# Two graph layers on one core: more direct rows on VectorE, list matrices and setup copies on ScalarE, square roots instead of powers from block 10, and the second product kept in two tensors

## The chip, the cores and the metric

The kernel runs on one core of one Trainium2 chip. The metric is the device time of one launch in microseconds (us). A core has five engines that each work through their own instructions in order: TensorE (PE in the profile, its weight loads PEld), VectorE (DVE), ScalarE (ACT), GpSimd (POOL) and SyncE (SP). Transfers between device memory and on-chip memory are started by SP or POOL and carried by 16 shared DMA engines.

## The reference

Two graph layers follow each other on 2708 nodes with 512 features. The adjacency matrix is dense in memory (2708 x 2708 float32), but only about 0.3% of it and its diagonal are nonzero.

```python
# layer 0
rowsum = adj.sum(axis=1)
d = where(rowsum > 0, rowsum ** -0.5, 0)
x = layernorm(x + relu(((d[:, None] * adj * d[None, :]) @ x) @ W + b))
# layer 1, four heads; A_self and A_neigh drop out of the softmax (they add one number to a whole row)
t = x @ W_node + b_node
feats = einsum('nd,hdf->hnf', t, K)
attn = softmax(s[:, :, None] - 1e10 * (1 - adj))        # over the neighbours
x = layernorm(x + relu(mean_h(attn @ feats)))
```

Because of the factor 1e10 a row's softmax puts all weight on its largest adjacency entry. Layer 1 is therefore one row of `u = h @ M + c` per node, where `h` is layer 0's output, `M` is `W_node @ mean(K)`, and the row is that of the largest entry. A check at the end branches to a dense version if the data break the assumptions; it doesn't run here.

## The kernel before, in words

The nodes are 21 full blocks of 128 rows and one of 20 rows. All instructions are placed by hand in one order (`manual_schedule`); on each engine they run in that order, each waiting for what it needs.

**Setup.** For each block `i` the program loads 128 rows of `adj` (1.35 MB, into one of 9 slots) and of `x`. `turn` transposes `x` on TensorE and a copy brings the result to on-chip memory (`sT`, line 219); `times` multiplies by `W`. `diagonal` (line 304, POOL) zeroes the diagonal, `sum_rows` (line 292, ACT) sums the rows, `root` makes `dinv` on POOL with a power. `value` (line 526) scales the product and stores it as `v_d`. `find` (lines 311 and 312, DVE) finds the eight largest entries of a third of each row, so that there are three searches a block. After a block's third search `under_0` (line 298, ACT) reads it a last time, and its slot is free for another load. 43 of the 66 searches stand before the main loop, the others within its first blocks. `weights` (line 490) makes `M` on TensorE.

**Lists.** For each block and each third, the largest entry is the *direct* one; the rest go into lists. `hot` (lines 392 and 397, DVE), `enlist` (line 410, TensorE) and `listed` (lines 422 to 426, DVE) compact the rest into six lists of up to 128 entries: a column, a row and a value each.

**Main loop.** Blocks 0 to 20 have nine chunks each, in the order direct, list, list, three times. For a chunk, POOL gathers 128 rows of `v_d` by an indirect DMA into a tile `g` (`fetch_chunk`, line 596). `small_matrix` makes a 128 x 128 matrix `s`: for a direct chunk a diagonal, on ACT (line 626), for a list chunk a matrix with one entry a row, on DVE (line 631). TensorE adds `s` times `g` to `acc` (`add_chunk`, line 650). In blocks of `BY_VECTOR` (11 to 17) the direct chunks have no matrix and no product: DVE adds the scaled `g` to the block's own row tile `vs` (line 640). Matrices are made, and gathers issued, 11 chunks ahead of use; after block 11 the gathers run up to 22 chunks ahead. There are 12 tiles `g`, and 12 more (`g2`) from block 8 on.

At a block's end `norm_1` (lines 682 to 702) adds up, adds `x` and starts the layer norm. Below block 17 (`EARLY`) `spread` and `norm_2` make the inverse root with a power on POOL (line 707), `nbs` follows on ACT (line 711), and `norm_3` scales on ACT (line 730). From block 17 on `root_1` and `root_2` make it from ACT's square root and four small DVE operations (lines 716 to 725). Chunk 2 of the next block finishes the norm; chunk 7 transposes `h` (`turn_h`), and chunk 5 of the block after that makes its `u` (`u_product`, line 228, then `u_store`, line 764). `u` is stored whole in `u_d`, and blocks 0 to 16 also in `u_e`.

**Rows that don't fit.** Some 128 rows with more entries than the lists hold are gathered whole (`l_a`) in block 10 and multiplied densely, block by block: `listed_turn` (line 959), its copy `l_t` on ACT (line 961), `listed_product` (line 968). They are handled as a block `L` of their own.

**Layer 1.** When `u` of blocks 0 to 16 and of `L` is there, `y_fetch` (line 1000, POOL) gathers each node's row of `u_e`; `y_1` (line 1012, DVE), `y_2` (line 1017, ACT), `root_1`, `root_2` and `y_3` finish the norm, and the block is stored. These pieces (`pieces_y`) are spread over the last chunks and the end. Nodes whose row lies in blocks 17 to 20 are *late*: their `h` is gathered from `h_d` (`to_read`), their `u` from `u_d` (`top_l`), and they are put into the output by indirect stores (`to_put`).

Of the kernel before, what the change touches and what calls it, by code (L numbers as in the profile page):

```python
# [39 lines left out]
F32 = mybir.dt.float32  # L40
# [15 lines left out]
DIRECT = 1  # L56
BY_VECTOR = range(11, 18)
FOUND = 7
# [3 lines left out]
def tile_two_graph_layers(  # L62
# [51 lines left out]
    v_d = dram.tile([N, D], F32, name="v_d")  # L114
    u_d = dram.tile([N, D], F32, name="u_d")
    u_e = dram.tile([EARLY * P, D], F32, name="u_e")
    h_d = dram.tile([N // P * P, D], F32, name="h_d")

# [300 lines left out]
    def listed(ib):  # L419

        t = search.tile([P, NL, 6], F32, name="sheet", bufs=6)
        nc.vector.tensor_copy(t, sheets.pop(ib)[:, : NL * 6].rearrange("p (n c) -> p n c", c=6))  # L422
        col = search.tile([P, NL], U32, name="l_col", bufs=6)
        val = search.tile([P, NL], F32, name="l_val", bufs=6)
        nc.vector.scalar_tensor_tensor(col, t[:, :, 1], float(P), t[:, :, 2], op0=ALU.mult, op1=ALU.add)
        nc.vector.tensor_reduce(val, t[:, :, 3:], axis=AX.X, op=ALU.add)
        lists[ib] = t[:, :, 0], col, val

# [93 lines left out]
    def value(i):  # L522

        pr = rows(i)
        vt = wpool.tile([P, D], F32, name="vt", bufs=3)
        nc.scalar.activation(vt[:pr], pos_w.pop(i)[:pr], AF.Copy, scale=dinv[:pr, i : i + 1])
        store(v_d, vt, i, nc.gpsimd if i < NB - 3 else nc.sync)
        if i == 0:
            nc.gpsimd.dma_start(out=u_d[full:N, :], in_=vt[: N - full])

# [7 lines left out]
    for i in range(NB):  # L538
# [3 lines left out]
        if i + 1 < NB:  # L542
            search_for(i + 1)
            diagonal(i + 1)
            xT[i + 1] = turn(xs.pop(i + 1), rows(i + 1), nc.vector.tensor_copy)
        pos_w[i] = times(xT.pop(i), pr, w_sb, po=p_acc.tile([P, D], F32, name="acc"))
# [6 lines left out]
        if 10 <= i < 10 + ND:  # L553
            turn_weight(i - 10)
        elif i == 15:
            b_columns()
        elif i == NB - 2:
            c_row = bias_1()
        elif i == NB - 1:
            pieces(c_3, c_row)  # L560
        for _ in range(2 if i else 1):
            if finds[0][0] <= i and len(finds) > 3 * (NB - 12):
                search_next()
# [28 lines left out]
    def by_vector(ib, c):  # L592
        return ib in BY_VECTOR and CHUNKS[c][0] == "d"

# [23 lines left out]
    def small_matrix(ib, c):  # L618
# [10 lines left out]
        else:  # L629
            row, _, val = lists[ib]  # L630
            nc.vector.tensor_scalar(  # L631
# [38 lines left out]
    def own_term(ib):  # L670

        pr = rows(ib)
        vs = own[ib][0]
        if not bias_on_pe(ib):
            nc.vector.scalar_tensor_tensor(
# [3 lines left out]
    def norm_1(n, pr, t, ac, vs, xr):  # L679

        if bias_on_pe(n):
            nc.vector.scalar_tensor_tensor(
# [6 lines left out]
        )  # L689
        if n < EARLY:  # L690
            spread(n, pr, t, xr)
        else:
            s = slice(n, n + 1)
            nc.vector.tensor_scalar(nms[:pr, s], tot[:pr, s], -1.0 / D, None, op0=ALU.mult)
            nc.scalar.activation(xr[:pr], t[:pr], AF.Square, bias=nms[:pr, s], accum_out=sqs[:pr, s])

# [59 lines left out]
    def u_store(ib):  # L756
# [10 lines left out]
        elif ib == EARLY - 1:  # L767
            later(1, lambda: put(ut, u_e[:, :], dl["own"][:, ib : ib + 1], EARLY * P))
        if ib >= NS - 2 and ib != L:
            put(ut, u_d[:, :], dl["own"][:, ib : ib + 1])  # L770
        elif ib != L:
            store(u_d, ut, ib)
        u_done.add(ib)
# [140 lines left out]
    def rank_4():  # L914
# [13 lines left out]
        nc.vector.tensor_copy(to_put, other)  # L928
        nc.vector.scalar_tensor_tensor(top_l, t[:, :, 2], float(P), t[:, :, 3], op0=ALU.mult, op1=ALU.add)
        nc.vector.scalar_tensor_tensor(put_own, flag, float(N), own_row, op0=ALU.mult, op1=ALU.add)  # L930
        dl.update(read=to_read, put=to_put, top=top_l, own=put_own)

# [42 lines left out]
    def listed_norm():  # L975
# [5 lines left out]
        )  # L981
        spread(L, P, t, dl["x"])

# [13 lines left out]
    def y_fetch(n):  # L997

        ys[n] = row_space()
        nc.gpsimd.indirect_dma_start(  # L1000
            out=ys[n],
            out_offset=None,
            in_=u_e[:, :],
            in_offset=bass.IndirectOffsetOnAxis(ap=idx[:, n : n + 1], axis=0),
            bounds_check=EARLY * P - 1,
            oob_is_err=False,
        )

    def y_1(n):
        t = h_of[n]  # L1010
        s = slice(n, n + 1)
        nc.vector.scalar_tensor_tensor(t, ys[n], 0.0, t, op0=ALU.max, op1=ALU.add, accum_out=tot[:, s])
        nc.vector.tensor_scalar(nms[:, s], tot[:, s], -1.0 / D, None, op0=ALU.mult)

    def y_2(n):
        s = slice(n, n + 1)
        nc.scalar.activation(ys.pop(n), h_of[n], AF.Square, bias=nms[:, s], accum_out=sqs[:, s])

    def y_3(n):
        (norm_3 if n % 2 else norm_v)(n, P, h_of[n])  # L1020


    GROUP = 3
    n_pieces = NS + 11
    early_y = [[] for _ in range(n_pieces)]
    for n in range(NS):
        last = n // GROUP * GROUP + GROUP - 1
        early_y[n].append(lambda n=n: y_fetch(n))
        early_y[n + 5].append(lambda n=n: (y_1(n), y_2(n)))
        if n == last:  # L1030
            early_y[last + 6].append(lambda n=n: root_1(n - GROUP + 1, n + 1))
            early_y[last + 7].append(lambda n=n: root_2(n - GROUP + 1, n + 1))
        early_y[last + 8 + n % GROUP].append(lambda n=n: (y_3(n), store(out, h_of[n], n)))

    def pieces_y(k):
        for _ in range(k):
            for f in early_y.pop(0) if early_y else ():
                f()


# [37 lines left out]
    for ib in range(NS):  # L1078
        pr = rows(ib)
        listing = []  # L1080
        for c in range(C):
# [17 lines left out]
            if c in (4, 8) and listing:  # L1099
                listed(listing.pop(0))  # L1100
            if finds and c in (1, 4, 7):
                search_next()
# [4 lines left out]
            if found_at is not None:  # L1107
                for f in plan.pop((ib - found_at, c), []):
                    f()
            if c == 2 and ib:  # L1110
                if ib - 1 < EARLY:
                    norm_2(ib - 1, ib, rows(ib - 1))
                    norm_3(ib - 1, rows(ib - 1), space(ib - 1))
                else:
                    root_1(ib - 1, ib)
                    root_2(ib - 1, ib)
                    norm_v(ib - 1, P, space(ib - 1))
                store(h_d, space(ib - 1), ib - 1)
# [5 lines left out]
            for k in sorted(products_u):  # L1124
                u_store(k)
            if c == (5 if ib <= EARLY else 1):
                for k in sorted(hTs):
# [7 lines left out]
            if dl.get("at") == n - 2:  # L1135
                norm_2(L, L + 1, P)
                norm_3(L, P, h_of[L])
                waiting_h.append(L)
            if L in h_of and "at" not in dl:
                dl["at"] = n  # L1140
            if "set" not in dl and u_done >= set(range(EARLY - 1)) | {L}:
                dl["set"] = n
                later(3, lambda: put(dl["u"], u_e[:, :], dl["put"][:, NLATE:], EARLY * P))
            if "go" not in dl and u_done >= set(range(EARLY)) | {L}:
                dl["go"] = n + 4
            if "put_l" not in dl and u_done >= set(range(NS - 2)) | {L}:
                dl["put_l"] = n
                later(4, lambda: put(dl["u"], u_d[:, :], dl["put"][:, NLATE:]))
            if n >= dl.get("go", n + 1) and (n - dl["go"]) % 4 != 3:
                pieces_y(1)  # L1150
            tick()
        if not finds and late is None:
# [9 lines left out]
            nc.scalar.copy(c_bc, po)  # L1162
        if 9 <= ib < 12:

            at = (EARLY - 1, NS - 2, NS - 1)[ib - 9]
            store(u_e if at < EARLY else u_d, space(ib - 9), at)
        if ib + 1 < NS:
# [3 lines left out]
    assert not finds and not plan and not products_l and "go" in dl and hot_next == NS  # L1171
    assert "put_l" in dl and not due and not products_u

    ib = NS - 1
    u_product(ib - 1)
    root_1(ib, ib + 1)
    pieces_y(1)
    root_2(ib, ib + 1)
    norm_v(ib, P, space(ib))
    store(h_d, space(ib), ib)  # L1180
    stir(8)
    turn_h(ib)
    u_store(ib - 1)
    u_product(ib)
    pieces_y(max(3, NS - 1 - (n_pieces - len(early_y))))
    pieces_y(2)
    for k in range(NLATE):
        h_of[L + 1 + k] = row_space()
        fetch(h_of[L + 1 + k], P, dl["read"][:, k : k + 1], h_d[:, :])
        if k == 2:  # L1190
            u_store(ib)
            pieces_y(1)
    pieces_y(2)

    order = [L] + [L + 1 + k for k in range(NLATE)]
    for n in order:
        ys[n] = row_space()
        k = NLATE if n == L else n - L - 1
        fetch(ys[n], P, dl["top"][:, k : k + 1], u_d[:, :])
        pieces_y(1)  # L1200
# [12 lines left out]

    def square(n):
        y_1(n)
        y_2(n)

    for n in order[: half + 1]:
        square(n)
        if n == first[-1]:  # L1220
            root_1(first[0], first[-1] + 1)
    root_2(first[0], first[-1] + 1)
    for n in first:
        y_3(n)
        rows_out(n)
    for n in order[half + 1 :]:
        square(n)
    root_1(second[0], second[-1] + 1)
# [150 lines left out]
```

## Time and profile before

| | us |
|---|---|
| median of 3 runs (512.05 to 519.46) | 513.81 |
| the profiled execution, device time | 516.84 |
| its span, first to last instruction | 515.1 |
| busy: TensorE / VectorE / ScalarE / GpSimd | 420.5 / 375.4 / 244.3 / 335.2 |
| first gather of the main loop issued | 142.7 |
| first product of the main loop | 151.0 |
| last gather of the main loop issued | 430.3 |
| block 20's layer norm begins (VectorE) | 464.4 |
| the last store's issue ends | 509.5 |

The span splits into the setup (to about 150 us), the main loop (to about 465 us) and an end of some 50 us, in which the last `u` is made, stored, and gathered again. A share of busy time over the whole span says little here, since the three have different limits; each is read by itself.

### The profile page before, as it was taken

To read this page: it belongs to the slowest core of one execution; us is meant where nothing else is said; L and a number is where in the kernel's file an instruction comes from. 1 tells how busy PE (TensorE), PEld (TensorE's weight loads), DVE (VectorE), ACT (ScalarE), POOL (GpSimd) and SP (SyncE) were. 2 spreads that over 40 slices of the span, in tenths; PEclk is the share of its full clock that TensorE was granted. 3 is DMA by queue.
4 is the path that set the end of the run, shared out by engine and by line. 5 is a ranking of instruction groups with operands and counts; after the bars stand their busy time and mean duration, and the time that the engine had idled before them with its cause. 6 is when DMAs were issued, how large, how long until landed. Compare 5 with 4: busy or idle time off the path is not lost. (4 is left out here: it accounts for less than half of the span.)

```text
span 515.1 us, 5634 instructions
## 1 busy us (share of the span) xinstructions
PE 420.5 (82%) x1431; PEld 200.9 (39%) x1431; DVE 375.4 (73%) x917; ACT 244.3 (47%) x413; POOL 335.2 (65%) x441
## 2 busy tenths in 40 slices
PE   4969859788979999999998799599898999976000
PEld 3424334343334444444444445244343444433000
DVE  2999999997887988888789938256345454777742
ACT  1598978779642544554532205112222251465631
POOL 6334543453677777777774778888778765745644
PEclk9998999989988999999999989899899799999555
DMA  7999999996276788898895899699899866776862
GB/s 228 424 398 419 396 350 347 372 357 257 93 224 192 234 256 291 302 291 277 267 327 177 267 392 382 212 346 322 284 307 315 300 198 222 238 235 226 296 202 98
DMA packets 54093, 145.79 MB, mean 283 GB/s; under 512 B 10771, under 2 KB 10771, under 8 KB 51216
## 3 DMA queue, kind: packets, MB, share of 16 engines
q0 software_dynamic: 21920, 68.94, 43.5%
q1 hardware_dynamic: 32132, 76.41, 39.3%
q8 instruction: 13, 0.21, 0.2%
q14 instruction: 28, 0.23, 0.1%
HBM read 117.59 MB, written 29.44 MB: 285 GB/s over the span
## 5 line engine op out<-in xcount | busy, mean ns | idle before, releaser
L650 PE MATMUL acc<-g,s 128*128 128x512 f32 x336 | 165.6, 623 | 3.1 <-DMA g<-v_d,l_col 3.1
L596 POOL DMA_INDIRECT g<-v_d,l_col x126 | 134.6, 1069 | 38.0 <-issue 20.4
L650 PEld LDWEIGHTS acc<-g,s 128*128 128x128 f32 x336 | 62.8, 199 | 70.5 <-issue 63.2
L228 PE MATMUL acc<-w_sb,sT 128*128 128x512 f32 (+1 forms) x176 | 85.5, 632 | 0.0
L228 PE MATMUL po<-m_sb,sT 128*128 128x512 f32 x176 | 82.6, 614 | 3.6 <-ACT sT L219 3.6
L596 POOL DMA_INDIRECT g<-v_d,cols x63 | 69.8, 1108 | 22.4 <-issue 10.2
L311 DVE MAX8 vals<-a 128x8 f32<-128x896 f32 (+2 forms) x66 | 71.8, 1088 | 1.0 <-ACT a L292 1.0
L312 DVE FIND_INDEX8 ats<-vals,a 128x8 uint32<-128x896 f32 (+2 forms) x66 | 72.0, 1091 | 0.0
L298 ACT ACTIVATE a<-a 128x2708 f32<-128x2708 f32 (+1 forms) x22 | 54.0, 2457 | 15.9 <-DVE ats L312 15.8
L292 ACT ACTIVATE a<-a 128x2708 f32<-128x2708 f32 (+1 forms) x22 | 54.0, 2456 | 13.4 <-POOL a L304 13.2
L228 PEld LDWEIGHTS po<-m_sb,sT 128*128 128x128 f32 x176 | 34.0, 197 | 46.5 <-issue 41.4
L228 PEld LDWEIGHTS acc<-w_sb,sT 128*128 128x128 f32 (+1 forms) x176 | 33.4, 200 | 36.2 <-issue 36.2
L631 DVE TENSOR_SCALAR s<-place,sheet,l_val 128x128 f32<-128x128 f32 x126 | 40.7, 354 | 4.2 <-PE acc L650 4.1
L219 ACT COPY sT<-tp 128x512 f32<-128x512 f32 x23 | 13.4, 583 | 62.7 <-PE tp L217 62.7
L304 POOL TENSOR_SCALAR_AFFINE_SELECT a<-a 128x128 f32<-128x128 f32 (+1 forms) x22 | 6.5, 295 | 55.8 <-DMA a<-in_adj_dram 49.5
L711 ACT ACTIVATE nbs<-nms,rss 128x1 f32<-128x1 f32 x18 | 5.3, 293 | 67.4 <-POOL rss L707 67.4
L422 DVE COPY sheet<-ls 128x36 f32<-128x36 f32 x21 | 4.0, 192 | 42.7 <-PE ls L410 42.7
L410 PEld LDWEIGHTS <-hot 128*128 128x128 bf16 x378 | 26.7, 161 | 18.3 <-issue 11.0
L217 PE MATMUL tp<-ident,x 128*128 128x128 f32 (+1 forms) x88 | 14.6, 291 | 21.9 <-DMA x<-in_x_dram 17.5
L410 PE MATMUL ls<-either,hot 128*128 128x12 bf16 x378 | 26.0, 203 | 4.7 <-DVE l_sheet L918 2.8
L1000 POOL DMA_INDIRECT g<-u_e,idx x21 | 23.6, 1122 | 7.2 <-issue 4.6
L392 DVE TENSOR_TENSOR hot<-place,places 128x2304 bf16<-128x2304 bf16 x21 | 28.2, 1344 | 0.0
(250 smaller groups left out, 566.7 us busy)
## 6 DMA issues: line engine op xcount, KB each, us to landing
a<-in_adj_dram SPq DMA_DIRECT2D x21, 1354.0 KB, 17.2
x<-in_x_dram SPq DMA_DIRECT2D x21, 256.0 KB, 12.5
vs<-v_d SPq DMA_DIRECT2D x21, 256.0 KB, 5.1
xr<-in_x_dram SPq DMA_DIRECT2D x21, 256.0 KB, 6.4
l_v<-v_d SPq DMA_DIRECT2D x21, 256.0 KB, 6.0
v_d<-vt POOLq DMA_DIRECT2D x19, 256.0 KB, 7.3
u_d<-ut SPq DMA_DIRECT2D x19, 256.0 KB, 4.2
u_e<-ut SPq DMA_DIRECT2D x16, 256.0 KB, 4.2
```

Source lines behind the costliest of these rows:

```text
L217: nc.tensor.transpose(ps[:, f, :pr], src[:pr, f * P : (f + 1) * P], ident[:pr, :pr])
L228: nc.tensor.matmul(po[:pr], sT[:, f, :pr], wt[:, f, :], start=(f == 0 and row_3 is None), stop=(f == ND - 1))
L292: nc.scalar.activation(a, a, AF.Copy, accum_out=sums[:pr, ib : ib + 1])
L298: nc.scalar.activation(a, a, AF.Relu, scale=-1.0, accum_out=bad[:pr, NB + ib : NB + ib + 1])
L311: nc.vector.max(out=vals[:pr, ib, t, :], in_=part)
L312: nc.vector.max_index(out=ats[:pr, ib, t, :], in_max=vals[:pr, ib, t, :], in_values=part)
L392: nc.vector.tensor_tensor(h_t, place_1, at[:, ib - lo, :].unsqueeze(1).to_broadcast([P, P, NE_1]), op=ALU.is_equal)
L410: nc.tensor.matmul(ls[:, t * 12 : t * 12 + 12], h_t[:, :, e], either[:, e].rearrange("p k c -> p (k c)"), start=(e == 0), stop=(e == NE_1 ...
L596: nc.gpsimd.indirect_dma_start(out=t[:pr], out_offset=None, in_=src, in_offset=bass.IndirectOffsetOnAxis(ap=ap, axis=0))
L631: nc.vector.tensor_scalar(s[:, :pr], place[:, :pr], row[:, t : t + 1], val[:, t : t + 1], op0=ALU.is_equal, op1=ALU.mult)
L650: nc.tensor.matmul(acc[ib][:pr], ss.pop((ib, c))[:k, :pr], g[:k], start=(first and not bias_on_pe(ib)), stop=(c == len(CHUNKS) - 1),)
L1000: nc.gpsimd.indirect_dma_start(out=ys[n], out_offset=None, in_=u_e[:, :], in_offset=bass.IndirectOffsetOnAxis(ap=idx[:, n : n + 1], axis=0 ...
```

## The change

- `BY_VECTOR` is now blocks 1 to 17. Below block 11 (`FREE`) only the second and third direct chunk go to DVE, the first stays a product. The block's own term, which in blocks below 9 was folded into the sum at the end, is made ahead by a `tensor_scalar`.
- List matrices are made on ACT in blocks 0 to 17 (in blocks 0 to 10 four of six): the absolute difference of column number and row, then `relu(val - val * difference)`. `listed` makes the two negated columns this needs.
- In the setup the copy of turned `x` goes from DVE to ACT. The bound on early searches is lifted: 47 instead of 43 stand before the main loop, and from block 3 on there are two a block instead of three.
- From block 10 (`ROOTS_AT`) the inverse root is made from ACT's square root, with `root_1` at chunk 2 and `root_2` at chunk 3; block `L` too.
- `u_d` holds rows of blocks 17 to 20 alone (532 rows). The 17 stores of earlier blocks into it go; those of 17 and 18, SP's before, become indirect stores on POOL. Block `L` is gathered from both tensors.
- The end is reordered: no layer-1 pieces in the last three chunks, one piece later between fetch and use, `u_store` of blocks 19 and 20 ahead of most pieces, 16 instead of 8 filling transposes (`stir`), two late fetches of `h` ahead of the last store.

```diff
-BY_VECTOR = range(11, 18)
+ROOTS_AT = 10
+BY_VECTOR = range(1, 18)
+FREE = 11
-    u_d = dram.tile([N, D], F32, name="u_d")
+    u_d = dram.tile([N - EARLY * P, D], F32, name="u_d")
...
-        lists[ib] = t[:, :, 0], col, val
+        minus_row, minus_val = t[:, :, 3], t[:, :, 4]
+        nc.vector.tensor_scalar(minus_row, t[:, :, 0], -1.0, None, op0=ALU.mult)
+        nc.vector.tensor_scalar(minus_val, val, -1.0, None, op0=ALU.mult)
+        lists[ib] = t[:, :, 0], col, val, minus_row, minus_val
...
-            xT[i + 1] = turn(xs.pop(i + 1), rows(i + 1), nc.vector.tensor_copy)
+            xT[i + 1] = turn(xs.pop(i + 1), rows(i + 1), nc.scalar.copy)
...
-            if finds[0][0] <= i and len(finds) > 3 * (NB - 12):
+            if finds[0][0] <= i:
                 search_next()
...
     def by_vector(ib, c):
-        return ib in BY_VECTOR and CHUNKS[c][0] == "d"
+        return ib in BY_VECTOR and CHUNKS[c][0] == "d" and (ib >= FREE or c > 0)
+
+    def by_scalar(ib, c):
+        return ib < BY_VECTOR[-1] + 1 and (ib >= FREE or CHUNKS[c][1] < 4)
...
-            row, _, val = lists[ib]
+            row, _, val, minus_row, minus_val = lists[ib]
+            if by_scalar(ib, c):
+                nc.scalar.activation(s[:, :pr], place[:, :pr], AF.Abs, bias=minus_row[:, t : t + 1])
+                nc.scalar.activation(
+                    s[:, :pr], s[:, :pr], AF.Relu, scale=minus_val[:, t : t + 1], bias=val[:, t : t + 1]
+                )
+                return
...
-        if not bias_on_pe(ib):
+        if bias_on_pe(ib):
+            if ib in BY_VECTOR:
+                nc.vector.tensor_scalar(vs[:pr], vs[:pr], self_d[:pr, ib : ib + 1], None, op0=ALU.mult)
+        else:
...
-        if bias_on_pe(n):
+        if bias_on_pe(n) and n not in BY_VECTOR:
...
-        if n < EARLY:
-            spread(n, pr, t, xr)
-        else: ...
+        (spread if n < ROOTS_AT else squares)(n, pr, t, xr)
...
-        if ib >= NS - 2 and ib != L:
-            put(ut, u_d[:, :], dl["own"][:, ib : ib + 1])
         elif ib != L:
-            store(u_d, ut, ib)
+            late_put = lambda: put(ut, u_d[:, :], dl["own_d"][:, ib : ib + 1], N - EARLY * P)
+            late_put() if ib >= NS - 2 else later(3, late_put)
...
-        (norm_3 if n % 2 else norm_v)(n, P, h_of[n])
+        (norm_3 if n % 3 else norm_v)(n, P, h_of[n])
...
-        early_y[n + 5].append(lambda n=n: (y_1(n), y_2(n)))
+        early_y[n + 6].append(lambda n=n: y_1(n))
...
-            if finds and c in (1, 4, 7):
+            if finds and c in ((1, 4, 7) if ib < 3 else (1, 5)):
...
-            if c == 2 and ib:
-                if ib - 1 < EARLY:
+            if c == 2 and ib > ROOTS_AT:
+                root_1(ib - 1, ib)
+            if c == (2 if ib <= ROOTS_AT else 3) and ib:
+                k = slice(ib - 1, ib)
+                if ib <= ROOTS_AT:
                     norm_2(ib - 1, ib, rows(ib - 1))
-                    norm_3(ib - 1, rows(ib - 1), space(ib - 1))
                 else:
-                    root_1(ib - 1, ib)
                     root_2(ib - 1, ib)
-                    norm_v(ib - 1, P, space(ib - 1))
+                    nc.scalar.activation(nbs[:, k], nms[:, k], AF.Copy, scale=rss[:, k])
+                norm_3(ib - 1, rows(ib - 1), space(ib - 1))
...
-            if n >= dl.get("go", n + 1) and (n - dl["go"]) % 4 != 3:
+            if n >= dl.get("go", n + 1) and (n - dl["go"]) % 4 != 3 and n < len(chunks) - 3:
                 pieces_y(1)
...
     u_product(ib - 1)
+    u_store(ib - 1)
     root_1(ib, ib + 1)
-    pieces_y(1)
     root_2(ib, ib + 1)
     norm_v(ib, P, space(ib))
     store(h_d, space(ib), ib)
-    stir(8)
+    stir(16)
     turn_h(ib)
-    u_store(ib - 1)
     u_product(ib)
-    pieces_y(max(3, NS - 1 - (n_pieces - len(early_y))))
-    pieces_y(2)
+    pieces_y(3)
+    for k in range(2):
+        late_h(k)
+    u_store(ib)
+    while n_pieces - len(early_y) < NS:
+        pieces_y(1)
+    ys[L] = row_space()
+    fetch_some(ys[L], dl["top"][:, NLATE:], u_e[:, :], EARLY * P)
+    for k in range(2, NLATE):
+        late_h(k)
```

## The prediction, made before the change was run

> **What bounds the kernel now.** I read the windows first: the limit changes from stage to stage. Columns: stretch and length, then busy time of TensorE, weight loads, VectorE, ScalarE and GpSimd, clock, DMA share, GB/s.
>
> ```profile
> 40.00:60.00 20.00, 18.98 (x54) 8.61 (x52) 19.72 (x30) 19.21 (x19) 11.21 (x32) 0.96 1.02 420
> 220.00:240.00 20.00, 20.00 (x66) 9.01 (x65) 17.70 (x34) 10.15 (x20) 16.02 (x17) 1.00 0.90 291
> 360.00:380.00 20.00, 17.71 (x60) 8.32 (x59) 8.29 (x19) 3.65 (x11) 16.14 (x15) 0.91 0.92 319
> ```
>
> In the setup (first line) the DMA, VectorE and ScalarE are full together. In blocks 5 and 6 (second line) TensorE has no gap: it bounds. At 360 to 380 us it has 2.3 us of gaps while VectorE and ScalarE are mostly idle. The waits say where those gaps come from (engine, what waits, what it waits for: total us, times, longest), and the timelines of ScalarE and TensorE show one:
>
> ```profile
> ACT nbs L711 <- POOL rss L707: 67.4, 16, 10.0
> PE po L959 <- ACT l_t L961: 12.1, 5, 5.5
> ...
> 320.60 0.25 ACT L961 COPY l_t<-po 128x128 f32<-128x128 f32 x1
> 330.86 0.29 ACT L711 ACTIVATE nbs<-nms,rss 128x1 f32<-128x1 f32 x1 [10.01 <-POOL rss L707]
> 331.91 0.24 ACT L961 COPY l_t<-po 128x128 f32<-128x128 f32 x1
> ...
> 332.20 0.47 PE L959 MATMUL po<-ident,l_a 128*128 128x128 f32 x1 [5.48 <-ACT l_t L961]
> ```
>
> The power (`rss`) stands in POOL's queue among gathers, `nbs` blocks ScalarE's queue for 10 us, and the copy of `l_t` behind it holds TensorE for 5.48 us. Five such stalls sum to 12.1 us, all in blocks 11 to 16. Between, at 258 to 298 us (blocks 8 to 10), VectorE is busy without a gap, so there it sets the pace. At the end:
>
> ```profile
> 456.90 1.88 PE L650 MATMUL acc<-g,s 128*128 128x512 f32 x4
> ...
> 463.72 0.68 DVE L686 TENSOR_TENSOR vs<-acc,vs 128x512 f32<-128x512 f32 x1
> ...
> 477.85 0.69 DVE L764 TENSOR_TENSOR ut<-po,c_bc 128x512 f32<-128x512 f32 x1
> ...
> 481.39 1.01 POOL L985 DMA_INDIRECT u_d<-ut,put_own  x1 [0.30 <-DVE vrs L717]
> 488.02 1.08 POOL L596 DMA_INDIRECT g<-u_d,top_l  x1 [2.80 <-issue]
> ```
>
> TensorE ends block 20 at 458.8; VectorE takes it up 4.9 us later, the block's `u` is added 13.4 us after the norm began (464.44), and the fetch of `u_d` goes 10.2 us after that. The gathers run ahead of TensorE (last gather 430.3), by 16 us in block 7 and by 28 us at the end, so TensorE and not POOL sets the main loop's end.
>
> **What the Trainium skill says.** "ScalarE: Activation LUTs", section "What ACT_TABLE_LOAD costs", puts an ACTIVATE with one per-partition operand at 280 ns + 0.833 ns an element, 387 ns for 128 columns, a second such operand at 93 ns more; the trace has 391 ns (`s`, line 626). "SBUF — State Buffer", section "SBUF: two separate sides", says that a VectorE operation in a fast mode locks GpSimd out of the port it writes descriptors through: in the trace a gather that begins at 342.06 beside a `hot` of 1.35 us takes 2.37 us, not 0.95. "Perfetto Trace Analysis", section "Summary: the profiler window per engine type", says that a software DMA's row ends with descriptor generation; so a gather's 0.95 us is POOL's time alone.
>
> **The change part by part**, against the profiled execution's span of 515.1 us (device time 516.84, so 1.74 lie outside it). Prices:
>
> ```profile
> L626 ACT ACTIVATE s<-ident,scaled 128x128 f32<-128x128 f32 x42 | 16.0, 391 | 7.1 <-PE acc L650 7.1
> L640 DVE SCALAR_TENSOR_TENSOR vs<-g,scaled,vs 128x512 f32<-128x512 f32 x21 | 15.7, 746 | 0.0
> L631 DVE TENSOR_SCALAR s<-place,sheet,l_val 128x128 f32<-128x128 f32 x126 | 40.7, 354 | 4.2 <-PE acc L650 4.1
> L707 POOL TENSOR_TENSOR rss<-sqs,half_neg 128x1 f32<-128x1 f32 x18 | 13.6, 758 | 7.5 <-ACT sqs L702 7.1
> ```
>
> *Setup, +0.8.* 20 copies go from VectorE (676 ns) to ScalarE (583); per step of 5.0 us VectorE loses 0.6 us and ScalarE gains 0.5. ScalarE has room (15 to 17 of 20 us busy from 60 to 120), and the DMA, full from 20 to 120, is unmoved. But the last turned `x`, ready at 118.4, now stands behind `under_0` (120.53 to 123.0), and its product comes 0.9 us later in a TensorE stretch without gaps; I take +0.8. Four more searches (4 × 2.2 us) fit into what VectorE saves (20 × 0.6). From below: −4, if VectorE's searches and not the DMA free the slots. From above: +7, if ScalarE falls behind by 20 × 0.5 and regains only 3.
>
> *Blocks 1 to 10.* Each loses two direct products of 2 × 0.43 us: 17.2 us of TensorE in all. VectorE gains 20 additions of 0.75 and loses 44 list matrices (0.28 back to back, 12.3 us). ScalarE loses 20 diagonals (0.39) and gains 44 list matrices of two dependent ACTIVATEs, about 0.8 each (0.39 + 0.48 less overlap): per block 7.0 becomes about 8.4 of 12.5 us. In blocks 1 to 7 TensorE needs 13.74 − 1.72 = 12.02 a block, and alone would gain 12. But the gather stream takes over: it runs at 12.6 a block (b5 205.81, b8 243.66), block b's power stands on POOL behind the gather of block b+2's fourth chunk, and `turn_h` in chunk 7 needs it. Gather (7, 7) goes at 241.14; with 4.8 to land and its products, and chunks after it, chunk 7 starts near 251.8, and the norm of block 7 begins at 255.3 instead of 260.08. So −4.8; bounds 0 and −12.
>
> *VectorE's stretch (blocks 8 to 10), +1.1.* Six additions (4.1), small operations of `listed` and of the ranking of late rows (1.8), less 14 list matrices × 0.27 (3.8): +2.1. One late product of block 10 goes: −0.9, rounded with it to +1.1 in the sum.
>
> *Roots from block 10, −12.1.* The power leaves POOL's queue; `nbs` now waits for five small VectorE operations, about 5 us after the norm rather than 11, so `l_t` is no longer late. 42 list matrices enter ScalarE's queue in blocks 11 to 17 (3.6 becomes about 8.3 of 13.5 a block) and could give back 2 to 3. Bounds 0 and −12.1; I take all. POOL saves 8 × 0.758 = 6.1 us, hidden unless POOL becomes the bound; 42 list matrices less on VectorE there (8.3 of 20 busy) are worth nothing.
>
> TensorE's end: 0.8 − 4.8 + 1.1 − 12.1 = −15.0, 458.8 to 443.8.
>
> *The end, −4.2.* VectorE's lag behind block 20: no pieces in the last three chunks, 9 `y_1` instead of 11 ahead; 4.9 becomes 2.5 (−2.4). Between norm and `u`, 3 `y_1` instead of 6: 13.4 becomes 10.5 (−2.9). Behind the put of `u`, POOL has 7 issues of 1.32 us, 9.2, where it had a shorter queue and a wait: 10.2 becomes 11.3 (+1.1). 17 stores of 256 KB leave SP and the DMA, whose share in the main loop is about 0.9; two become indirect stores on POOL (1.0 each), hidden. From `u_d`'s fetch to the end 27.1 us as before.
>
> POOL's check: its last gather moves from 430.3 to about 419.5 (stall of 6.0 at 281 down to 1.9, and 6.1 of powers); 26 row fetches × 1.32 from 424.5 end at 458.8, and `ut` of block 20 is ready near 457. Balanced: POOL may set the end.
>
> Sum: −15.0 − 4.2 = −19.2. Span 495.9, device time 497.6; the medians stand to that execution as 513.81 to 516.84 (0.9941): 494.7. Forecast **495**.
>
> **Rivals.**
>
> *POOL sets the end* (0.18). The balance above says how near this is. Then the earlier end of TensorE only waits in POOL's queue: of 19.2 about 10 remains, 513.81 − 10 = **504**. For it: POOL is 16 of 20 us busy and only 0.30 us lies between gathers. Against: it loses 6.1 us of powers.
>
> *The gathers give way and the setup too* (0.15). If VectorE's searches free the slots, setup −4 instead of +0.8; if gathers follow TensorE because its tiles come free sooner, blocks 1 to 7 gain 12 and not 4.8. Together −12.0 more: **483**. For it: TensorE at 20.00 of 20. Against: the 12.6 us a block of gathers.
>
> *ScalarE's queue becomes the bound* (0.06; slower). Its place: the setup, where it is 19.21 of 20 busy at 40 to 60, and blocks 1 to 7, where matrices, searches' `under_0` and norms share one order. Setup +7 and not +0.8 (+6.2); 1.3 a block for seven blocks (+9) instead of −4.8; and the list matrices ahead of `l_t` keep the 12.1. −19.2 + 6.2 + 13.8 + 12.1 = +12.9: **527**. It decides once ScalarE needs more than TensorE's 13.7 a block; 8.4 is far from it.
>
> **Numbers.** The forecast case has 0.58, POOL 0.18, the larger gain 0.15, ScalarE 0.06, the rest 0.03 lies between no change and POOL's case. Range: **483 to 507**, from the larger gain to just past POOL's case. The measurement tells about 2% from no change: 503.5 and 524.1 bound that. Half of POOL's case (0.09) and most of the rest fall within 2%, and some of the forecast's own spread: faster 0.81, same 0.13, slower 0.06.
>
> **What would show it.** Right: no wait of `nbs` on POOL from block 10, none of line 959's matmul on `l_t` over 1 us; block 7's norm near 256 and block 20's last product near 444; VectorE takes it up within 3 us; `u_d` fetches near 469. Wrong: ScalarE at 95% in blocks 2 to 7, or matrices `s` named as what TensorE waits for; the first product of the main loop past 155; a put of `u` that POOL reaches more than 5 us after `ut`; gathers of block 8 before 238, which would be the larger gain.

## The result, and the profile after

The changed kernel takes 496.12 us (median of 4 runs, 495.26 to 496.34) against 515.62 us (median of 4 runs, the three of the table above and one more): a ratio of 0.9617, 95% interval [0.954, 0.9695]. Some executions of a kernel fall into a slower state; ratios, here and below, compare the others alone, medians take all. The profiled execution has a span of 494.5 us (device time 496.23). The forecast was 495 us, with 483 to 507 around it. The spans differ by 20.6 us where the sum had said 19.2, but the terms of that sum came out quite differently, as the stages show.

The same three windows as before the change (TensorE, weight loads, VectorE, ScalarE, GpSimd, clock, DMA share, GB/s):

```profile
40.00:60.00 20.00, 15.36 (x48) 6.91 (x47) 19.66 (x29) 19.64 (x20) 10.60 (x29) 1.00 1.02 419
220.00:240.00 20.00, 20.00 (x65) 9.04 (x65) 18.06 (x34) 12.47 (x29) 16.13 (x16) 1.00 0.87 276
360.00:380.00 20.00, 20.00 (x72) 9.90 (x71) 12.37 (x36) 12.07 (x34) 15.26 (x16) 1.00 0.99 358
```

TensorE is still full in the early blocks, with less to do in each, and now it is full at 360 us too, where it had gaps of 2.3 us and a granted clock of 0.91. ScalarE has risen to 12 of 20 us: it is far from being a bound in the loop. The stalls on `l_t` (line 959 before, 994 now) that summed to 12.1 us are gone from TensorE's waits altogether, and the waits of `nbs` on POOL's power have shrunk from 67.4 us to:

```profile
ACT nbs L731 <- POOL rss L727: 13.4, 5, 5.1
```

By stage (a block's norm is counted from VectorE's row that adds `x`, line 687 before and 706 after; its lag behind TensorE is measured to the row before it, so that 0.7 us stand in no row of the table):

| stage | before | after | gain | forecast |
|---|---|---|---|---|
| start to the first product of the loop | 151.0 | 155.7 | +4.7 | +0.8 |
| from there to block 7's norm | 109.1 | 101.3 | −7.8 | −4.8 |
| block 7's norm to block 10's | 48.2 | 47.7 | −0.6 | +1.1 |
| block 10's norm to block 11's | 10.4 | 14.7 | +4.4 | 0 |
| block 11's norm to block 16's | 87.2 | 70.4 | −16.8 | −12.1 |
| block 16's norm to TensorE's last product of block 20 | 52.9 | 52.0 | −0.9 | 0 |
| VectorE's lag behind it | 4.9 | 0.0 | −4.9 | −2.4 |
| block 20's norm to its `u` added | 13.4 | 10.5 | −2.9 | −2.9 |
| `u` added to the first fetch of `u_d` | 10.2 | 14.5 | +4.3 | +1.1 |
| that fetch to the end | 27.1 | 27.0 | −0.1 | 0 |

**The stage of the roots.** Two windows of the kernel before (the whole stage, and 2.5 us behind the stall of 5.48 us) and, below, the stage in the changed kernel:

```profile
318.68:405.91 87.23, 75.12 (x269) 36.59 (x268) 41.48 (x96) 18.53 (x56) 70.29 (x67) 0.93 0.89 302
332.50:335.00 2.50, 2.50 (x4) 0.98 (x4) 0.00 (x0) 0.27 (x1) 1.89 (x3) 0.50 0.82 241
```

```profile
319.39:389.84 70.45, 70.45 (x271) 35.72 (x270) 39.78 (x105) 41.12 (x111) 51.97 (x54) 0.99 0.97 342
```

Of the 16.8 us, 12.1 are the five stalls: 87.23 less 75.12 is all the time in which TensorE stood idle there. The other 4.7 are TensorE's own busy time, for practically the same matmuls. Behind three of the stalls, those of 5.48, 2.29 and 2.27 us, the granted clock falls to 0.50 for 3 to 7 us; behind the two of 1.02 and 1.05 us it doesn't. What lowers it is not shown: in `c_before`, a second profile of the kernel before, it falls behind a stall of 5.86 us but not behind two of 2.39 and 2.27, and the stage takes 84.1 us.

**The late start.** ScalarE's and TensorE's timelines at the end of the setup, before the change and after it:

```profile
139.26 0.68 ACT L526 ACTIVATE vt<-acc,dinv 20x512 f32<-20x512 f32 x1 [2.06 <-POOL dinv L264]
148.11 2.46 ACT L298 ACTIVATE a<-a 128x2708 f32<-128x2708 f32 x1
...
133.53 14.05 PE L490 MATMUL po<-h_early 128*128 128x512 f32 x32
151.00 5.32 PE L650 MATMUL acc<-g,s 128*128 128x512 f32 x8 [3.10 <-DMA g<-v_d,l_col]
```


```profile
139.83 2.46 ACT L300 ACTIVATE a<-a 128x2708 f32<-128x2708 f32 x1 [3.33 <-DVE ats L314]
142.20 0.19 ACT L300 ACTIVATION_READ_ACCUMULATOR a<-a 128x1 f32 x1
142.29 0.66 ACT L531 ACTIVATE vt<-acc,dinv 20x512 f32<-20x512 f32 x1
142.86 1.03 ACT L496 COPY m_sb<-po 128x512 f32<-128x512 f32 x2
...
152.81 2.46 ACT L300 ACTIVATE a<-a 128x2708 f32<-128x2708 f32 x1
...
143.47 8.81 PE L495 MATMUL po<-h_early 128*128 128x512 f32 x16 [2.14 <-ACT m_sb L496]
155.70 5.40 PE L666 MATMUL acc<-g,s 128*128 128x512 f32 x8 [3.10 <-ACT s L635]
```

With the bound on early searches lifted, block 13's third search is made in the last step of the setup's loop, and its `under_0` (line 300 after, 298 before) stands in ScalarE's queue between the last two `vt`; in the kernel before it came behind the copies of `M`, at 148.11. It waits 3.33 us for VectorE's search; the last `v_d`, the first gather (145.76 instead of 142.73) and the copies of `M` wait behind it, and TensorE loses 2.14 us on a copy and then runs at a granted clock of 0.50 for some 3 us. So the weights (`M`) end 4.7 us later. A second `under_0` at 152.81, block 14's, which had come within block 0, stands before the first matrix `s`, which TensorE waits for.

**The cost of the moved root.** Some of what the root saves is paid for at its first use, for block 10's norm in block 11 (VectorE, ScalarE, TensorE):

```profile
312.11 0.16 DVE L742 RECIPROCAL rss<-sds 128x1 f32<-128x1 f32 x1 [4.85 <-ACT sds L736]
...
307.93 2.45 ACT L980 ACTIVATE l_a<-l_a 128x2708 f32<-128x2708 f32 x1
310.29 0.19 ACT L980 ACTIVATION_READ_ACCUMULATOR l_a<-l_a 128x1 f32 x1
310.49 1.28 ACT L736 ACT_TABLE_LOAD   x1
...
314.47 1.29 PE L412 MATMUL ls<-either,hot 128*128 128x12 bf16 x18 [2.76 <-DVE either L399]
```

The first square root comes here instead of at 424 us, so its table is loaded here, behind the pass over `l_a`. VectorE's queue stops 4.85 us on the root, of which the load is 1.28; the `hot` behind it is late, TensorE waits 2.76 us for the lists' input, and its granted clock is 0.50 from 314.5 to 319 us. In the kernel before, `hot` ran beside that pass and TensorE did not wait:

```profile
310.24 2.44 ACT L945 ACTIVATE l_a<-l_a 128x2708 f32<-128x2708 f32 x1
...
311.29 1.35 DVE L392 TENSOR_TENSOR hot<-place,places 128x2304 bf16<-128x2304 bf16 x1
...
315.23 1.23 PE L410 MATMUL ls<-either,hot 128*128 128x12 bf16 x18
```

The Trainium skill ("ScalarE: Activation LUTs", section "What ACT_TABLE_LOAD costs") gives 1283 ns for the load, as here; the drain of 1380 ns that it adds is not seen, since the row before ends at the load's start and the root follows at 311.78.

**The end.** TensorE, VectorE and POOL:

```profile
439.91 1.88 PE L666 MATMUL acc<-g,s 128*128 128x512 f32 x4
...
441.83 0.69 DVE L705 TENSOR_TENSOR vs<-acc,vs 128x512 f32<-128x512 f32 x1 [1.19 <-PE acc L666]
...
453.02 0.69 DVE L784 TENSOR_TENSOR ut<-po,c_bc 128x512 f32<-128x512 f32 x1
...
447.42 1.19 POOL L1020 DMA_INDIRECT u_d<-ut,own_d  x1 [4.08 <-DVE rss L745]
455.87 1.45 POOL L1020 DMA_INDIRECT u_d<-ut,own_d  x1 [0.30 <-DVE nbs L747]
467.50 1.01 POOL L1039 DMA_INDIRECT g<-u_d,top_d  x1 [0.30 <-issue]
```

VectorE now waits 1.19 us for TensorE, where it had come 4.9 us late. POOL stands still for 4.08 us before block 19's put and then has a full queue behind block 20's: seven issues between that put and the fetch.

### The profile page after: what moved, and what is told of

Read it like the earlier page. It is cut to its first block, busy times and chain, and to the rows that moved or that the text cites. A ratio compares the mean times of both kernels' runs of the same rounds, so it can differ in the third digit from the quotient of the medians.

```text
span 494.5 us, 5746 instructions
## 1 busy us (share of the span) xinstructions
PE 401.4 (81%) x1399; PEld 193.8 (39%) x1399; DVE 368.0 (74%) x929; ACT 317.6 (64%) x587; POOL 318.3 (64%) x436
## 5 line engine op out<-in xcount | busy, mean ns | idle before, releaser
L605 POOL DMA_INDIRECT g<-v_d,l_col x126 | 127.3, 1010 | 42.7 <-issue 22.0
L666 PE MATMUL acc<-g,s 128*128 128x512 f32 x296 | 148.8, 628 | 3.1 <-ACT s L635 3.1
L605 POOL DMA_INDIRECT g<-v_d,cols x63 | 65.1, 1033 | 26.1 <-issue 13.1
L230 PE MATMUL po<-m_sb,sT 128*128 128x512 f32 x176 | 79.9, 597 | 0.9 <-ACT sT L221 0.9
L666 PEld LDWEIGHTS acc<-g,s 128*128 128x128 f32 x296 | 55.4, 201 | 61.6 <-issue 49.8
L230 PEld LDWEIGHTS po<-m_sb,sT 128*128 128x128 f32 x176 | 33.0, 191 | 42.1 <-issue 37.8
L221 ACT COPY sT<-tp 128x512 f32<-128x512 f32 (+1 forms) x44 | 25.4, 576 | 34.9 <-PE tp L219 34.8
L643 ACT ACTIVATE s<-s,l_val,sheet 128x128 f32<-128x128 f32 x86 | 42.4, 493 | 2.9
L412 PE MATMUL ls<-either,hot 128*128 128x12 bf16 x378 | 26.0, 203 | 15.2 <-DVE either L399 10.5
L412 PEld LDWEIGHTS <-hot 128*128 128x128 bf16 x378 | 26.5, 161 | 27.2 <-DVE either L399 13.8
L642 ACT ACTIVATE s<-place,sheet 128x128 f32<-128x128 f32 x86 | 33.4, 388 | 0.0
L656 DVE SCALAR_TENSOR_TENSOR vs<-g,scaled,vs 128x512 f32<-128x512 f32 x41 | 30.5, 743 | 0.0
## 6 DMA issues: line engine op xcount, KB each, us to landing
a<-in_adj_dram SPq DMA_DIRECT2D x21, 1354.0 KB, 17.8
x<-in_x_dram SPq DMA_DIRECT2D x21, 256.0 KB, 12.4
```

The costliest lines, as they stand in the source:

```text
L230: nc.tensor.matmul(po[:pr], sT[:, f, :pr], wt[:, f, :], start=(f == 0 and row_3 is None), stop=(f == ND - 1))
L412: nc.tensor.matmul(ls[:, t * 12 : t * 12 + 12], h_t[:, :, e], either[:, e].rearrange("p k c -> p (k c)"), start=(e == 0), stop=(e == NE_1 ...
L605: nc.gpsimd.indirect_dma_start(out=t[:pr], out_offset=None, in_=src, in_offset=bass.IndirectOffsetOnAxis(ap=ap, axis=0))
L642: nc.scalar.activation(s[:, :pr], place[:, :pr], AF.Abs, bias=minus_row[:, t : t + 1])
L643: nc.scalar.activation(s[:, :pr], s[:, :pr], AF.Relu, scale=minus_val[:, t : t + 1], bias=val[:, t : t + 1])
L656: nc.vector.scalar_tensor_tensor(vs, g, scaled[:, ib, CHUNKS[c][1], 0:1], vs, op0=ALU.mult, op1=ALU.add)
```

## Experiments

**One chip apart.** The first four edits and one repeat of the changed kernel ran on a chip on which the kernel before took 537 to 541 us and not 515; the later ones ran where it took 516.5 to 517. Chip and hour changed together, so these runs do not tell which of them it was. Each run is read against its own chip.

`e1_defer`: `under_0` of blocks 13 and 14 goes into block 0.

```diff
...
-            under_0(ib)
+            (held.append if holding[0] else under_0)(ib)      # from i = NB - 2 to the loop
...
+            if ib == 0 and c in (2, 6):
+                if held:
+                    under_0(held.pop(0))
```

> The changed kernel with one edit: under_0 of blocks 13 and 14 (ScalarE, 2.46 us each) is held back until chunks 2 and 6 of block 0; the searches stay where they are. Theory A: the 4.7 us by which the first product of the main loop came later in the changed kernel (155.7 against 151.0) is ScalarE's queue: under_0(13) waits for VectorE's search until 139.8, and the last v_d, the copies of M and the first matrices stand behind it. Then the first product is back at 150 to 152 and the 4 to 5 us reach the end, since TensorE has no gap in blocks 1 to 7: about 491.5 us. Rival B: the stretch of blocks 8 to 10, or POOL at the end, swallows what the start gains: 495 to 497 us. Rival C: the delay is TensorE's or the DMA's own: first product stays at 155.

`e2_products` and `e3_powers`: one constant each.

```diff
-BY_VECTOR = range(1, 18)
+BY_VECTOR = range(11, 18)
```

> The changed kernel with BY_VECTOR back at blocks 11 to 17: the 20 direct products of blocks 1 to 10 are on TensorE again, their matrices on ScalarE; all else stays. Theory A: TensorE alone sets the pace of blocks 1 to 7, 12.1 us a block with the change; each block gets 1.7 us back, less some relief of VectorE in blocks 8 to 10: norms 13.8 us apart, total +9 to +12, 505 to 508 us. Theory B (the step of the prediction): gathers and powers limit these blocks near their pace, so that the two products are worth only about 5: 501 us. Theory C: POOL sets the end, so that little of it arrives: 497 to 499 us.

```diff
-ROOTS_AT = 10
+ROOTS_AT = 17
```

> The changed kernel with ROOTS_AT at 17 instead of 10: the inverse roots of blocks 10 to 16 are powers on POOL again, nbs waits for them; all else stays. Theory A: the stalls of TensorE on l_t come back (12.1 us in the kernel before), and the list matrices now in ScalarE's queue are late with them: +12 to +17, 508 to 513 us, with waits of nbs on POOL of up to 10 us. Theory B: the stalls went because list matrices and pace changed, not because of the root: within 3 us of 496, no stall of line 994's matmul on l_t over 1 us.

`e4_vector_lists`: no list matrix on ScalarE.

```diff
-        return ib < BY_VECTOR[-1] + 1 and (ib >= FREE or CHUNKS[c][1] < 4)
+        return False
```

> The changed kernel with all list matrices on VectorE again (by_scalar always false), 86 of them off ScalarE; all else stays. Theory A: VectorE, 17 to 19.6 of 20 us busy in blocks 2 to 10, gets 0.28 us for each: four a block, 44 in blocks 0 to 10; it becomes the bound there and the total rises by 4 to 8: 500 to 504 us. Theory B: in blocks 1 to 7 VectorE still has room, only blocks 8 to 10 lose their 3.4: 498 to 500 us. Theory C: the matrices on ScalarE cost as much by standing before l_t and the norms as they save: 494 to 497 us.

Measured: 537.76, 549.7, 554.48 and 542.45 us, beside 540.72 for the kernel before; ratios 1.0014 [0.9982, 1.0046] for `e1_defer`, 1.0292 [1.0205, 1.0379] for `e3_powers`, 0.9951 [0.9894, 1.0007] for `e4_vector_lists`, none for `e2_products`. Against 0.9617 all four look like losses of everything the change brought, which made the chip itself the question.

`c_after`, the changed kernel unedited:

> The changed kernel itself once more, unedited, as the base of the comparison: in the profiles of the first four edits every engine now and then waits 5 to 14 us for something that the trace names only as remote, and the kernel before took 540.7 us beside them, not 515. Theory A: those waits belong to the chip or to the hour, not to the edits: the changed kernel shows them too and lies 1 to 4% below the kernel before, so that the edits are to be read against it and not against 496 us. Theory B: they come from the edits: the changed kernel has none and is again at 0.96 of the kernel before.

Measured: 535.6 us, ratio 0.9953 [0.9909, 0.9998]. As theory A says, the waits are there without any edit; the gain is half a per cent, less than its 1 to 4. Lists' sums on TensorE and the copy of `sheet` on VectorE that waits for them, in block 5 of the first profile of the changed kernel and, below it, in block 4 of this one:

```profile
229.37 1.22 PE L412 MATMUL ls<-either,hot 128*128 128x12 bf16 x18
230.63 0.20 DVE L424 COPY sheet<-ls 128x36 f32<-128x36 f32 x1 [1.46 <-PE ls L412]
```

```profile
224.03 1.22 PE L412 MATMUL ls<-either,hot 128*128 128x12 bf16 x18
231.92 0.20 DVE L424 COPY sheet<-ls 128x36 f32<-128x36 f32 x1 [7.16 <-PE acc L666]
```

The copy follows 0.04 us after the end of the sums in the first, 6.67 us in the second, while nothing stands before it on VectorE. Such waits are spread over this chip's profiles, 67 us of them under the name remote in `c_after`, summed over the engines, none in the first profiles. So on this chip the change is worth only half a per cent. Beside `c_after`, `e3_powers` is about 3.4% slower (18 us; TensorE waits 15.8 us on `l_t` at two lines, 3.6 in `c_after`); `e2_products` is slower too, without an interval; `e4_vector_lists` can't be told from it; `e1_defer` has its first product at 148.8 instead of 153.7 us and is no faster. Sizes from this chip are not used further.

`c_before`, the kernel before once more:

> The kernel before, unedited, profiled beside the others on the chip where it takes 537 to 541 us. Theory A: signals of TensorE reach the other engines late on this chip (in the changed kernel there, the copy of sheet after the lists' sums waits up to 6.7 us beyond the recorded end; 0.03 us in the first profile), and since the changed kernel has less slack between its engines, it loses 39 us to them and the kernel before only 22: the trace shows such waits (remote, 5 to 14 us), but fewer, and TensorE's blocks 1 to 7 stay near 14 us apart. Theory B: the kernel before loses as many waits, and the difference lies elsewhere.

Measured: 520.57 us, one run, on the quiet chip, with no wait named remote. The question it was made for, how the kernel before meets those waits, stays open.

`b_roots`, one part of the change alone on the kernel before:

```diff
...
+            if c == 2 and ROOTS_AT <= ib - 1 < EARLY:
+                root_1(ib - 1, ib)
+            if ib and c == (3 if ROOTS_AT <= ib - 1 < EARLY else 2):
...
+                if ROOTS_AT <= ib - 1 < EARLY:
+                    root_2(ib - 1, ib)
+                    nc.scalar.activation(nbs[:, k], nms[:, k], AF.Copy, scale=rss[:, k])
+                    norm_3(ib - 1, rows(ib - 1), space(ib - 1))
```

> The kernel before with one part of the change alone: the inverse roots of blocks 10 to 16 from ScalarE's square root and VectorE (root_1 at chunk 2, root_2, nbs and norm_3 at chunk 3); list matrices stay on VectorE. Theory A: the 12.1 us of TensorE's waits on l_t go, and since TensorE ends the main loop, 10 to 13 us of them reach the end: 0.975 to 0.98 of the kernel before. Theory B: without the products of blocks 1 to 10 gone, POOL's gathers or the end take over: 0.99 to 1.0. Where the profile has waits of line 959's matmul on l_t over 3 us in blocks 12 to 16, the root was not their cause.

Measured: 508.52 us beside 516.84, ratio 0.9858 [0.9795, 0.9921]: 8 us, less than theory A's 10 to 13. No wait of line 960's matmul on `l_t` is left, and blocks 12 to 16 are 13.4 to 14.0 us apart, TensorE without a gap: the root was the cause of the stalls. From block 11's norm to block 16's it is 69.5 us, 17.8 less than before. Two losses stand against this. Block 11 takes 15.5 us instead of 10.4, with the same waits of VectorE and TensorE at the first square root as in the changed kernel, though here ScalarE makes no list matrix:

```profile
313.72 0.16 DVE L723 RECIPROCAL rss<-sds 128x1 f32<-128x1 f32 x1 [4.84 <-ACT sds L717]
...
316.36 1.28 PE L411 MATMUL ls<-either,hot 128*128 128x12 bf16 x18 [3.04 <-DVE either L398]
```

And part of the gain is lost again in block 17, on ScalarE, TensorE and VectorE:

```profile
402.01 0.29 ACT L712 ACTIVATE nbs<-nms,rss 128x1 f32<-128x1 f32 x1 [3.06 <-POOL rss L708]
...
403.96 1.11 PE L218 MATMUL tp<-ident,l_h 128*128 128x128 f32 x4 [3.72 <-ACT sT L220]
...
407.87 0.20 DVE L423 COPY sheet<-ls 128x36 f32<-128x36 f32 x1 [6.46 <-PE ls L411]
```

Block `L`'s power is still on POOL in this kernel, and the same chain forms once more behind it: block 17 takes 19.8 us, 15.5 in the kernel before. The change moves that root too, and there block 17 takes 15.0.

`e5_tail`: POOL's last issues in another order.

```diff
...
     u_product(ib - 1)
+    ahead(3)                 # three row fetches of u_e, on POOL alone
     u_store(ib - 1)
...
-    pieces_y(3)
-    for k in range(2):
-        late_h(k)
+    ahead(3)
+    pieces_y(3)
     u_store(ib)
...
-    for k in range(2, NLATE):
+    for k in range(NLATE):
```

> The changed kernel with POOL's last issues in another order: three row fetches of u_e ahead of the put of block 19 (where POOL waited 4.1 us in the changed kernel's profile) and three ahead of the put of block 20, the five fetches of h_d behind it; VectorE's and ScalarE's order stays. Theory A: POOL's queue between the last put and the fetches of u_d sets the end (11.6 us there), and these come 4 to 5 us earlier after the last put than before, so that the whole is 3 to 5 us (0.6 to 0.9%) faster. Theory B: what follows the fetches, VectorE and ScalarE finishing the rows, sets the end: within 1 us of the changed kernel.

`e5_both`: this and `e1_defer` together.

> The changed kernel with both edits, under_0 of blocks 13 and 14 held back into block 0, and POOL's last issues reordered. Theory A: the two add: first product of the main loop 5 to 7 us earlier, the end 3 to 5 us shorter, 8 to 10 us in all, 1.5 to 2% below the changed kernel. Theory B: the earlier start is lost again in blocks 8 to 10, where VectorE sets the pace, or in late signals: not more than the reordered end alone.

Measured: 496.19 us (ratio 0.9625 [0.9562, 0.9688]) and **490.4 us (0.9516 [0.9451, 0.9581])**. By the medians the new order alone can't be told from the changed kernel. The profiled execution of `e5_tail`, the fastest of its four, has a shorter end all the same: 49.0 us from block 20's norm instead of 52.0 (50.2 in `e5_both`). Its fetches go 9.7 us after the last put instead of 11.6, and 3.8 us earlier after that norm; 0.8 of this is lost again, because VectorE still has rows in its queue when they land. POOL in `e5_tail`:

```profile
454.79 1.02 POOL L1020 DMA_INDIRECT u_d<-ut,own_d  x1 [1.43 <-DVE ut L784]
...
464.48 1.00 POOL L1050 DMA_INDIRECT g<-u_d,top_d  x1 [0.30 <-issue]
...
478.81 1.01 POOL L1020 DMA_INDIRECT out_dram<-g,to_put  x1 [6.78 <-SPq L1286]
```

From fetch to first output it is 14.3 us, 13.5 in the changed kernel and 15.8 in `e5_both`; VectorE, which waited 2.19 us for such a fetch in the changed kernel, takes the late rows up at 472.46, eight us after this one's issue, without waiting. So in the changed kernel POOL's queue came last, with VectorE close behind it. Whether the whole gains from the new order stays open: the end of that one profile speaks for theory A, the medians for theory B, and four runs between 494.06 and 497.3 us do not settle 3 us. The two kernels differ in the held-back `under_0` alone, and their runs lie apart (489.72 to 492.32 for `e5_both`): it is worth 5.8 us. TensorE in `e5_both`:

```profile
134.22 14.00 PE L497 MATMUL po<-h_early 128*128 128x512 f32 x32
148.15 0.39 PE L255 MATMUL acc<-b,every 3*128 3x512 bf16 x1
149.20 3.70 PE L669 MATMUL acc<-g,s 128*128 128x512 f32 x8 [0.66 <-ACT s L638]
```

The weights run through, and the first product is 6.5 us earlier than in the changed kernel's first profile, and 1.8 earlier than in the kernel before, where one `under_0` stood ahead of it too. Most of that arrives: `e5_both` beats both kernels, though it is short of theory A's 8 to 10 us. On the other chip the same edit alone brought nothing (`e1_defer`); here it was not run alone.

`e6_products`, `e6_vector_lists` and `c2_after` repeat the edits of `e2_products` and `e4_vector_lists`, and the changed kernel, on the quiet chip.

> As the second edit, BY_VECTOR back at blocks 11 to 17, once more: its first run fell on a chip with 5 to 14 us waits of another kind, which hide what it is worth. Theory A: TensorE alone sets the pace of blocks 1 to 7, so that the norms are again 13.7 us apart and not 12.1: +11 there, up to 2 back from VectorE in blocks 8 to 10: 9 to 11 us above the changed kernel. Theory B (the prediction's step: gathers and powers nearly as slow as TensorE): +5. Theory C: absorbed later, under 3.

> As the fourth edit, all list matrices on VectorE, once more for the same reason. Theory A: VectorE, 17 to 19.6 of 20 us busy in blocks 2 to 7, becomes the bound with four matrices more a block (1.1 us): norms 12.6 or more apart, and blocks 8 to 10 lose 3 to 4 more: 6 to 9 us above the changed kernel. Theory B: VectorE still has room in blocks 1 to 7, only the stretch of blocks 8 to 10 grows: +2 to +4. Theory C: the matrices on ScalarE cost what they save: within 1.5 us.

> The changed kernel, unedited, as the base for the two others on the same chip: about 0.962 of the kernel before, first product of the main loop at 155 to 156 us and norms 12.0 to 12.5 us apart in blocks 1 to 7, where the chip shows none of the 5 to 14 us waits; near 0.995 where it does.

Measured: 504.29 us (0.9777 [0.9691, 0.9864]), 504.66 us (0.9756 [0.9673, 0.9839]) and 496.71 us (0.963 [0.9561, 0.97]). The windows of `c2_after`, `e6_products` and `e6_vector_lists`, in this order:

```profile
220.00:240.00 20.00, 19.93 (x65) 8.85 (x64) 18.10 (x35) 12.25 (x28) 16.22 (x16) 1.00 0.86 270
```

```profile
220.00:240.00 20.00, 20.00 (x71) 9.34 (x71) 13.85 (x30) 11.68 (x31) 15.81 (x17) 1.00 0.87 265
```

```profile
220.00:240.00 20.00, 20.00 (x76) 9.29 (x74) 19.11 (x39) 7.28 (x16) 15.95 (x17) 1.00 0.84 276
```

With the products back, the norms of blocks 2 to 7 are 13.2 to 13.8 us apart, not 11.6 to 13.5, and block 7's norm is at 263.6 instead of 257.4: TensorE's work sets that pace. In all the 20 products are worth 7.6 us, between the two expectations; VectorE, relieved of its additions, gets 4 us back from block 7 to block 10 (44.7 instead of 48.6) and loses most of that again in block 11. With the list matrices on VectorE, block 7's norm stays at 257.8: at 19.1 of 20 us VectorE still had room. The loss comes later: 4.5 us more between the norms of blocks 7 and 11, as theory B has the place, and 3.6 more after block 20's (54.9 us to the end instead of 51.3), 8 us in all by the medians. Why the end is longer, where no matrix is made any more, is not shown.

What no run takes apart: the 17 stores that are gone, and the new order of the end as a whole.

## Why the prediction was right

Its time is right, and so are its main mechanisms: the stalls go with the root (`b_roots`), and fewer products shorten blocks 1 to 7 (`e6_products`). That the sum came within 1.4 us of the span is luck: most of its terms were off, in ways that cancelled.

- *Roots, −12.1.* Right in mechanism. The stage gained 16.8: the 12.1 of the five stalls, and 4.7 of TensorE's own time at a lower granted clock, which the sum does not have. "I take all" left out what the moved root itself adds, 4.4 us in block 11. Together that is −12.4, and so the term looks exact.
- *VectorE's stretch, +1.1.* Measured −0.6 for blocks 8 to 10 (+0.3 in `c2_after`). The loss of 4.4 us in block 11 belongs to the root, as `b_roots` shows; neither the table load nor the wait behind it was in the sum. "Busy without a gap" said a little too much: VectorE worked 36.8 of the 40 us from 258 to 298. That it sets the pace there in the changed kernel, `e6_products` bears out.
- *Setup, +0.8.* Measured +4.7; the first product at 155.7 is one of the prediction's own signs of being wrong. The term for the copies of turned `x` was right: in `e5_both`, where only `under_0` is moved away, the weights end at 148.15, 0.6 after the kernel before's 147.52. What failed is "Four more searches (4 × 2.2 us) fit into what VectorE saves": counted as VectorE's time alone, and not with the `under_0` that the third search of a block issues into ScalarE's queue. The rival "ScalarE's queue becomes the bound" had the engine, but not the cause: it is not ScalarE's load over the setup that held things up. The last `vt` comes 3.8 us later than in `e5_both` because one `under_0` stands ahead of it: 2.5 us of work, and a wait of 3.33 us instead of the 2.06 that was there anyway.
- *Blocks 1 to 7, −4.8.* Measured −7.8. "But the gather stream takes over" did not hold in the first profile of the changed kernel: in blocks 3 to 7 TensorE ran its 12.0 us a block alone. The late start, with gathers already ahead, made room for that. In `e5_both`, whose first product comes 6.1 us earlier than that of `e5_tail` (149.2 and 155.3), the same blocks take 12.3 to 13.2 us, TensorE has short waits on gathers and norms, and only 3.4 of the 6.1 us are left at block 7's norm (252.4 and 255.8). Even with the late start block 7 takes 13.5 us in `c2_after` and `e5_tail`, with a wait of TensorE on a gather. The limit was near, and the late start hid most of it; at block 11 5.7 us are left again. The errors of these two terms are in large part one.
- *The end, −4.2.* Measured −3.6 from TensorE's last product on: VectorE's lag went altogether (−4.9, not −2.4), and POOL's queue cost 4.3, not 1.1, since the two fetches of `h` stand before the last put and nothing filled the 4.08 us before block 19's. "Balanced: POOL may set the end" fits the profile of `e5_tail`. The last gather was misread: 430.33 is the last but one in the kernel before, the last goes at 434.14, and at 420.43 after the change.

Of the rivals, neither the larger gain nor POOL's 504 us came about.

## What to carry to other kernels

When an edit moves an instruction, count what that instruction releases or issues on the other engines' queues, too: here four searches that fitted into VectorE's time put two ScalarE instructions, one of them waiting, ahead of the start of the loop, and keeping them out of the setup gained 5.8 us. A shared in-order queue is repaired by position as well as by speed: a root moved from POOL's queue to ScalarE's and VectorE's frees the one and can stall the others at its first use. A stall can cost more than its length where the clock falls behind it. A sum that fits is no proof of its terms; compare stage by stage, because a late start and a faster stage behind it are easily one and the same thing.

## What had not been expected of the hardware

One chip ran the same two kernels in 537 and 536 us, and a gain of 3.8% shrank to 0.5%. Its profiles show the other engines taking up TensorE's results late: in the pair of rows above 6.67 us after their recorded end, against 0.04 us in the first profile. Whether TensorE ended later than its records say, or its signals travelled late, these runs do not tell: the ends of matmuls are modelled.

Nor was it expected that waits of TensorE come with a lower clock behind them: 0.50 for 3 to 7 us behind waits of 2.14 and 2.76 us in the changed kernel and of 5.48, 2.29 and 2.27 us in the kernel before. At half the clock, 3 to 7 us are worth an estimated 1.5 to 3.5 us of TensorE's work. It did not follow every such wait.
